# Two quads of state sums at a time, nine u tiles, and a front half worked off half by half

## The chip, the cores and the metric

The kernel runs on one core of a Trainium2 chip. The core has a matrix engine (TensorE, PE in the profile), a vector engine (VectorE, DVE), a scalar engine (ScalarE, ACT), a pool engine (GpSimd, POOL) and a queue that issues transfers (SyncE, SP). The metric is the time on the device in microseconds. Before the change it is 3439.42 us, the median of three runs that lie between 3437.82 and 3448.25 us.

## The reference: what is computed

Eight images of 384 channels and 32 x 32 = 1024 positions go through one layer. The first half of it is a state space block ("Mamba" style), followed by a two-layer perceptron; the second half is a feed-forward part with sign-binarised weights and outputs scaled by a maximum over one image. Cut to what matters:

```
t = layernorm(layernorm_c(x)) * ln_w + ln_b
xm, z = split(t @ in_proj_w.T)                    # 2 x 768 columns
xc = silu(conv3(xm) + conv_b)                     # causal, 3 taps
dt, Bm, Cm = split(xc @ x_proj_w.T, [24, 40])     # 24 + 16 + 16 columns
dt = softplus(dt @ dt_proj_w.T + dt_proj_b)       # 768 columns
h_t = exp(dt_t * A) * h_(t-1) + dt_t * xc_t * B_t # 768 x 16 states, 1024 steps
y_t = sum over the 16 states of h_t * C_t
y = (y + xc * D) * silu(z)
t = gelu((y @ out_proj_w.T) @ mlp_w1.T + mlp_b1) @ mlp_w2.T + mlp_b2
x = x + t
# feed-forward, for the first five images; the others get zeros from it
h = quantise(layernorm(x) @ sign(W1 - mean).T + b1)    # maximum over the image
x = x + quantise(gelu(h) @ sign(W2 - mean).T + b2)
```

All arithmetic is in fp32.

## The kernel before

The program first writes down every operation of all images with its reads, writes and an estimated cost. A list scheduler (`Plan.run`) then plays the operations through a model of the five queues, and the order in which it takes them becomes the fixed order of instructions on each engine. Every buffer belongs to a ring of so many slots; an operation can be placed only when a slot is free in the model. When the model's TensorE would be idle for over 0.7 us it places small "spare" products with no use but to keep that engine running.

```
MM = 0.86          # model's cost of one 128x128x512 fp32 product (two passes)
SWITCH = 0.34      # model's cost of going over to the state sums and back
BATCH = 1          # quads of states that are summed at a time
SLACK = 1.0        # added in the model to what waits for the sums
...
"front": ring("front", 2), "t_f": ring("t_f", 2), "w_f": ring("w_f", 4),
"dt_r": ring("dt_r", 3), "dtx_r": ring("dtx_r", 3), "u": ring("u", 6),
"da": ring("da", 2, psum), "y": ring("y", 1, psum),
"yg": ring("yg", 1), "hid": ring("hid", 2), "t_b": ring("t_b", 1), "w_b": ring("w_b", 4),
"w6": ring("w6", 2), "w6_n": ring("w6_n", 2), "res": ring("res", 3),
"mm": ring("mm", 3, psum),
```

**The scan** (`scan`, `scan_tile`). The 16 states of a channel are four quads of four. A tile holds 32 channels x 4 states on the 128 partitions and 1024 positions. ScalarE makes `da = exp(dt * A)`, GpSimd `u = dtx * B`, VectorE scans `h = da * h + u`, then VectorE (three tiles of four) or GpSimd (one of four) multiplies by C into `u`, and TensorE adds the four states of each channel with a 128 x 32 matrix of ones and zeros, `fold`:

```
for m in range(DI // per_unit):            # a unit: 2 tiles for each of 4 quads
    py = self.piece("y", [P, T], "py")
    ...
    for q in range(NQUAD):
        hcs = []
        for i, js in enumerate(tiles):
            self.scan_tile(hcs, ...)       # each takes one u tile until it is summed
        batch.append((q, hcs))
        if len(batch) < BATCH:
            continue
        def sums(py=py, batch=batch):
            for q, hcs in batch:           # 4 products of 512 columns for each quad
                for p0, hc in parts:
                    nc.tensor.matmul(py.real[p0 : p0 + DQ, :], self.fold, hc,
                                     start=(q == 0), stop=(q == NQUAD - 1))
        with self.plan.lane(-1):
            add("PE", SWITCH + BATCH * MM, sums, ...)
```

There are 6 x 12 units of whole images and 2 x 2 x 6 units of the first and last image, whose scan runs in two halves of 512 positions with the state carried over; 96 units, 384 quads.

**The front** (`s1`) of an image, each half of 512 positions:

```
ts = [normed(half) for half in range(2)]   # load, two norms in one, scale and bias
for half, cols in enumerate(HALVES):
    t = ts[half]
    # 6 times: in_proj product with weights from ring w_f, conv on ScalarE and VectorE
    # silu; store xc
    if half:
        gate(0)                            # z = silu of the other 6 in_proj products
    # x_proj product with self.x_w; store rows of B and C
    # 6 dt_proj products with self.dt_w; softplus; dtx = dt * xc on GpSimd; store both
    if half:
        gate(1)
```

Image 1 alone uses the rings t_n, w_b, yg and hid for its front. Constants that stay in memory for the whole program are `self.x_w` (128 x 768), `self.dt_w` (128 x 768) and `self.spread` (128 x 512), which copies a norm's scale to all partitions and feeds the spare products.

**The back** (`s3`): out_proj (`p_out`), first perceptron product with weights from w_b (`p_h`), gelu, second product (`p_o`), residual in a `res` tile. **The feed-forward part** (`ffn`): `p_y<-tn` products with weights from w_b, each result through a `res` tile to memory, `p_y<-gf` products, two maxima by `quant_scale`, which spreads a column over a diagonal:

```
def spread_out():
    nc.vector.tensor_reduce(m1.real, mx.real, AX.X, ALU.max)
    nc.vector.tensor_scalar_mul(diag.real, self.ident, m1.real)
add("DVE", 0.4, spread_out, ...)
```

Of the kernel before, what the change touches and what calls it, by code (L numbers as in the profile page):

```python
# [26 lines left out]
F32 = mybir.dt.float32  # L27
AF = mybir.ActivationFunctionType
# [42 lines left out]

MM = 0.86
SWITCH = 0.34
BATCH = 1
SIGNAL = 0.1
IDLE = 0.7
EARLY = 2
PATIENCE = 0.0
SLACK = 1.0
LOAD_TABLE = 1.29  # L80


def c_act(n):
    return 0.22 + n * 0.00084
# [233 lines left out]
class Layer:  # L318
    def __init__(self, ctx, tc, a, out):
        self.tc, self.nc, self.a, self.out = tc, tc.nc, a, out  # L320
        self.plan = Plan()

        def pool(name, **kw):
            return ctx.enter_context(tc.tile_pool(name=name, bufs=1, **kw))

        self.const = pool("const")
        sbuf, psum, dram = pool("sbuf"), pool("psum", space=PSUM), pool("dram", space=DRAM)

        def ring(tag, bufs, where=sbuf):
            def make(shape, name):  # L330
                return where.tile(shape, F32, tag=tag, name=name, bufs=bufs)

            return Ring(make, bufs)

        self.rings = {

            "front": ring("front", 2), "t_f": ring("t_f", 2), "w_f": ring("w_f", 4),
            "dbc": ring("dbc", 1), "halo": ring("halo", 2),

            "dt_r": ring("dt_r", 3), "dtx_r": ring("dtx_r", 3), "u": ring("u", 6),  # L340
            "xr": ring("xr", 1), "zr": ring("zr", 1), "state": ring("state", 1),
            **{f"bc{i}": ring(f"bc{i}", 1) for i in range(2 * NQUAD)},
            "da": ring("da", 2, psum), "y": ring("y", 1, psum),

            "yg": ring("yg", 1), "hid": ring("hid", 2), "t_b": ring("t_b", 1), "w_b": ring("w_b", 4),
            "w6": ring("w6", 2), "w6_n": ring("w6_n", 2), "res": ring("res", 3),

            "t_n": ring("t_n", 2), "small": ring("small", 12),

            "mm": ring("mm", 3, psum), "sq": ring("sq", 2),  # L350
            "rstd": ring("rstd", 2),
        }

        def handed(name, shape):
            return Fixed(dram.tile(shape, F32, name=name))

        self.dram = {}
        for b in range(B):
            for name in ("dt", "dtx"):
                self.dram[name, b] = handed(f"{name}_d{b}", [DI, L])  # L360

            for name in ("xc", "z", "yg"):
                self.dram[name, b] = handed(f"{name}_d{b}", [NP, P, T])
            self.dram["rows", b] = handed(f"rows_d{b}", [2 * NS, L])
            if b < NQ:
                self.dram["mid", b] = handed(f"mid_d{b}", [C, L])
                self.dram["y1", b] = handed(f"y1_d{b}", [P, KH, L])
        self.bin = {
            "W1": handed("bin_w1", [KH, P, KC, P]), "W2": handed("bin_w2", [KC, P, KH, P]),
        }  # L370
        self.constants()

        self.plan.spare = self.piece("mm", [P, T], "spare")
        self.plan.fill = lambda: self.nc.tensor.matmul(
            self.plan.spare.real[:, : 2 * P], self.ones, self.spread[:, :2, :], start=True,
            stop=True,
        )

    def piece(self, ring, shape, name):
# [4 lines left out]
    def constants(self):  # L384
        nc, a, const = self.nc, self.a, self.const
        self.ones = const.tile([P, P], F32, name="ones")
        nc.vector.memset(self.ones, 1.0)
        self.ident = ident = const.tile([P, P], F32, name="ident")
        make_identity(nc, ident)

        self.fold = const.tile([P, DQ], F32, name="fold")
        nc.vector.tensor_reduce(
            self.fold, ident.rearrange("p (d n) -> p d n", n=SQ), AX.X, ALU.add
        )

        self.spread = const.tile([P, G, P], F32, name="spread")
        for g in range(G):
            nc.vector.tensor_copy(
                self.spread[:, g, :], ident[:, g * DQ : g * DQ + 1].to_broadcast([P, P])
            )  # L400
        self.edge = const.tile([P, KD, 2], F32, name="edge")
        self.eps_m = const.tile([P, 1], F32, name="eps_m")
        nc.vector.memset(self.eps_m, E1 * E2)
        self.eps_f = const.tile([P, 1], F32, name="eps_f")
        nc.vector.memset(self.eps_f, E_FFN)

        def vec(name, k):
            v = const.tile([P, k], F32, name=f"v_{name}")
            nc.scalar.dma_start(v, a[name])
            return v  # L410

        self.ln_w, self.ln_b, self.mlp_b2 = vec("ln_w", KC), vec("ln_b", KC), vec("mlp_b2", KC)
        self.conv_b, self.dt_b = vec("conv_b", KD), vec("dt_proj_b", KD)
        self.d_pair, self.d_unit = vec("D_pair", NP), vec("D", KD)
        self.mlp_b1 = vec("mlp_b1", KH)
        self.b1, self.b2 = vec("b1", KH), vec("b2", KC)
        self.conv_w = const.tile([P, KD, 3], F32, name="conv_w")
        nc.scalar.dma_start(self.conv_w, a["conv_w"])
        self.a_neg = const.tile([P, NJ * NQUAD], F32, name="a_neg")
        nc.scalar.dma_start(self.a_neg, a["A_log"])  # L420
        nc.scalar.activation(self.a_neg, self.a_neg, AF.Exp)
        nc.vector.tensor_scalar_mul(self.a_neg, self.a_neg, -1.0)
        self.x_w = const.tile([P, KD, P], F32, name="x_w")
        nc.scalar.dma_start(self.x_w, a["x_proj_w"])
        self.dt_w = const.tile([P, DI], F32, name="dt_w")
        nc.scalar.dma_start(self.dt_w, a["dt_proj_w"])

    def load(self, to, view, src, r=(), size=0, cost=0.4):  # L430
# [45 lines left out]
    def norm(self, t, eps, scale):  # L476
# [40 lines left out]

        def spread():
            for g in range(G):
                nc.tensor.matmul(  # L520
                    p_r.real[:, g * TG : (g + 1) * TG], self.spread[:, g, :], rstd.real,
                    start=True, stop=True,
                )

        add("PE", MM, spread, r=[rstd], w=[p_r])
# [6 lines left out]
    def s1(self, b):  # L532
# [31 lines left out]
                    )  # L564
            return t

        def gate(half):
            t = ts[half]
            z = self.piece(r_z, [P, KD, T], "z")
            for m in range(KD):  # L570
                w = self.weights(r_w, KC, a["in_proj_w"][KD + m])
# [6 lines left out]
                     r=[], w=all_z, table="silu")  # L578
            by_pair("z", half, z[0])

        ts = [normed(half) for half in range(2)]
        for half, cols in enumerate(HALVES):
            t = ts[half]


            xc = self.piece(r_x, [P, KD, T], "xc")
# [32 lines left out]
                     r=[], w=all_m, table="silu")  # L619
            by_pair("xc", half, xc[0])  # L620

            if half:
                gate(0)


            p_dbc = self.piece("mm", [P, T], "p_dbc")

            def x_proj(xc=xc, p_dbc=p_dbc):
                for k in range(KD):
                    nc.tensor.matmul(  # L630
                        p_dbc.real, self.x_w[:, k, :], xc.real[:, k, :],
                        start=(k == 0), stop=(k == KD - 1),
                    )

            dbc = self.piece("dbc", [P, T], "dbc")
            add("PE", KD * MM, x_proj, r=all_m, w=[p_dbc], claim=[dbc])
            add("ACT", 0.59, lambda dbc=dbc, p_dbc=p_dbc: nc.scalar.copy(dbc.real, p_dbc.real),
                r=[p_dbc], w=[dbc])
            d = self.dram["rows", b]
# [1 line left out]
                       4 * 2 * NS * T)  # L641
            dt = self.piece(r_x, [P, KD, T], "dt")
            for k in range(KD):
                i = k % DTC * DQ
                pd = self.piece("mm", [P, T], "p_dt")
                add("PE", MM / 2, lambda i=i, k=k, pd=pd, dbc=dbc: nc.tensor.matmul(
                    pd.real, self.dt_w[i : i + R, k * P : (k + 1) * P], dbc.real[i : i + R, :],
                    start=True, stop=True,
                ), r=[dbc], w=[pd], claim=[dt])
                self.act(  # L650
                    lambda k=k, dt=dt: dt.real[:, k, :], lambda pd=pd: pd.real, AF.Identity,
                    c_act(T), r=[pd], w=[dt[k]], bias=self.dt_b[:, k : k + 1],
                )
# [6 lines left out]
            all_dt = [dt[k] for k in range(KD)]  # L660
            self.store_all("dt", b, half, dt, all_dt)
            self.store_all("dtx", b, half, xc, all_m)
            if half:
                gate(1)

    def store_all(self, name, b, half, t, parts):
        d = self.dram[name, b]
# [124 lines left out]
    def scan_tile(self, hcs, cols, n, dt_r, dtx_r, bq, cq, state, half, on_pool):  # L792
# [22 lines left out]
            ), r=[da, u] + ([state[cols[0]]] if half else []), w=[to])  # L815
        if half == 0:
            c0, step = cols[0], cols[1] - cols[0]
            add("ACT", 0.25, lambda: nc.scalar.copy(
                state.real[:, c0 : c0 + step + 1 : step], to.real[:, :, n - 1]
            ), r=[to], w=[state[c0]])  # L820
        if on_pool:
            add("POOL", 2.36, lambda: nc.gpsimd.tensor_mul(u.real, u.real, spread(cq)),  # L822
                r=[cq], w=[u])
# [151 lines left out]
    def quant_scale(self, mx, n):  # L975
# [4 lines left out]
        q = self.piece("small", [P, 4], "q")  # L980
        diag, p_max = self.piece("sq", [P, P], "diag"), self.piece("mm", [P, P], "p_max")

        def spread_out():
            nc.vector.tensor_reduce(m1.real, mx.real, AX.X, ALU.max)
            nc.vector.tensor_scalar_mul(diag.real, self.ident, m1.real)

        add("DVE", 0.4, spread_out, r=[mx[k] for k in range(n)], w=[m1, diag])

        add("PE", 0.25, lambda: nc.tensor.matmul(
            p_max.real, self.ones, diag.real, start=True, stop=True  # L990
# [130 lines left out]
def _laid_out(i):  # L1121
# [25 lines left out]
        rows[k * DQ : k * DQ + R] = xw[:R]  # L1147
        a["dt_proj_w"][k * DQ : k * DQ + R] = dw.T
    rows[DTC * DQ :] = xw[R:]
    a["x_proj_w"] = rows.reshape(P, KD, P).transpose(2, 1, 0)  # L1150

    a["D_pair"] = np.tile(np.asarray(i[c + "D"]).reshape(NP, DP).T, (2, 1))
    w2 = blocks(i[c + "mlp_w2"])
# [29 lines left out]
```

## Time and profile before

| what | value |
|---|---|
| time, median of three | 3439.42 us |
| profiled span | 3444.9 us |
| busy PE, DVE, ACT, POOL | 3302.8, 2885.8, 2019.7, 2655.3 us |
| mean granted TensorE clock | 0.975 of full |
| moved by transfers | 746.30 MB, mean 217 GB/s |
| first and last scan instruction | 111.6 us, 3338.0 us |
| sums: instructions, busy | 3072, 427.9 us |
| spare products: instructions, busy | 522, 128.4 us |

One fp32 product is two instructions on TensorE. Their ends are modelled and overlap the next start, so the distance from one start to the next tells what a product costs, and the busy time overstates it. A group of instructions has one line with its count, its busy time, the mean of one, and the idle time of the engine just before it with what ended most of that. "L454" is the line of a helper that emits nearly all dense products; they are told apart by the names of the tiles. The table by stage that is used below is cut at the last operation of each image's scan, so each of its rows is the time in which one image is scanned while the other engines work on the front of a later image and the back of an earlier one.

### The profile page before, as it was taken

Reading aid. Unit: us, or ns where it says so; the run is one execution under the profiler, and the core shown is the slowest. Engines: PE = TensorE matmul, PEld = TensorE weight load, DVE = VectorE, ACT = ScalarE, POOL = GpSimd, SP = SyncE. Lnnn points to the kernel's source line nnn. Section 1 sums busy time; section 2 is a strip of 40 time slices with the busy share of each in tenths; the row PEclk is TensorE's granted clock in tenths of the full one; section 3 lists DMA queues with packets and bytes.
Section 4 is the critical chain, followed back from the end, with each engine's and each line's share of the span. In section 5 each row is a group of like instructions: output and inputs, shape, how many; then the busy total and the mean of one; then the engine's idle time right before and its main releaser. Section 6 shows DMA issues by size and latency. Waiting matters only on the chain.

```text
span 3444.9 us, 32879 instructions
## 1 busy us (share of the span) xinstructions
PE 3302.8 (96%) x10500; PEld 1326.3 (38%) x10500; DVE 2885.8 (84%) x2193; ACT 2019.7 (59%) x2295; POOL 2655.3 (77%) x1288
## 2 busy tenths in 40 slices
PE   8888898999999999999999999999899999999999
PEld 3333433434343334333333333333333433333344
DVE  3577789899899989789989989899998899789870
ACT  4676567556666565554565656655576554555541
POOL 1778777777897968689777888788898779878850
PEclk9889899999999999999999999999999999999999
DMA  5876757667686557765588665986577666766542
GB/s 192 259 237 210 242 179 231 200 207 248 228 285 200 198 191 259 240 215 188 206 270 278 221 204 184 304 248 215 177 269 250 199 201 208 238 190 206 182 138 69
DMA packets 363965, 746.30 MB, mean 217 GB/s; under 512 B 34832, under 2 KB 103952, under 8 KB 363792
## 3 DMA queue, kind: packets, MB, share of 16 engines
q1 hardware_dynamic: 361776, 743.31, 66.6%
q8 instruction: 84, 1.38, 0.2%
q10 hardware_dynamic: 2016, 0.88, 0.1%
q14 instruction: 89, 0.73, 0.1%
HBM read 560.56 MB, written 183.50 MB: 216 GB/s over the span
## 4 chain that ended last, share of the span: by engine, by line
PE 61%; DVE 12%; DMA 8%; ACT 8%; POOL 5%; issue 5%; SPq 1%; DVEq 0%; POOLq 0%; ACTq 0%
PE p_y L454 14%; PE p_o L454 11%; PE p_h L454 10%; PE py L745 7%; DVE da L812 7%; PE p_out L454 6%; PE p_in L454 4%; PE p_z L454 4%; ACT da L470 3%; POOL u L808 2%; DVE u L825 2%; PE p_dbc L630 2%; ACT L470 1%; PE p_sum L483 1%; DMA dt_r<-dt_d 1%
## 5 line engine op out<-in xcount | busy, mean ns | idle before, releaser
L808 POOL TENSOR_TENSOR u<-dtx_r,bc 128x1024 f32<-128x1024 f32 x768 | 1796.8, 2359 | 493.7 <-PE py L745 418.9
L812 DVE TENSOR_TENSOR_SCAN da<-da,u 128x1024 f32<-128x1024 f32 (+1 forms) x576 | 1163.9, 2021 | 187.3 <-ACT da L470 113.0
L470 ACT ACTIVATE da<-dt_r,a_neg 128x1024 f32<-128x1024 f32 (+1 forms) x960 | 903.1, 946 | 687.8 <-DVE u L825 571.8
L825 DVE TENSOR_TENSOR u<-da,bc 128x1024 f32<-128x1024 f32 x576 | 703.2, 1221 | 25.2 <-DVE da L812 0.9
L454 PE MATMUL p_h<-t,w_b 128*128 128x512 f32 x1152 | 519.9, 601 | 12.2 <-ACT g L470 9.4
L454 PE MATMUL p_o<-g,w 128*128 128x512 f32 x1152 | 513.8, 598 | 1.2 <-DMA w<-in_mlp_w 1.0
L822 POOL TENSOR_TENSOR u<-u,bc 128x1024 f32<-128x1024 f32 x192 | 452.7, 2358 | 66.6 <-DVE u L812 46.1
L745 PE MATMUL py<-u,fold 128*32 128x512 f32 x3072 | 427.9, 611 | 15.7 <-POOL u L822 15.4
L812 DVE TENSOR_TENSOR_SCAN u<-da,u 128x1024 f32<-128x1024 f32 (+1 forms) x192 | 384.3, 2011 | 45.8 <-ACT da L470 29.8
L454 PE MATMUL p_y<-gf,w_n 128*128 128x512 f32 x720 | 328.9, 610 | 12.7 <-DMA w_n<-bin_w 8.2
L454 PEld LDWEIGHTS p_h<-t,w_b 128*128 128x128 f32 x1152 | 212.2, 190 | 315.0 <-issue 252.0
L454 PE MATMUL p_y<-tn,w_b 128*128 128x512 f32 x720 | 328.4, 605 | 1.0 <-ACT dt L470 0.8
L454 PEld LDWEIGHTS p_o<-g,w 128*128 128x128 f32 x1152 | 213.6, 190 | 299.9 <-issue 288.2
L470 ACT ACT_TABLE_LOAD x223 | 286.1, 1283 | 8.4 <-DVE xc L601 4.7
L454 PE MATMUL p_out<-yg,w 128*128 128x512 f32 x576 | 267.3, 616 | 16.8 <-DMA yg<-yg_d 9.6
L454 PE MATMUL p_in<-t,w_f 128*128 128x512 f32 x504 | 232.3, 608 | 10.3 <-ACT halo L596 6.0
L454 PE MATMUL p_z<-t,w_f 128*128 128x512 f32 x504 | 231.1, 607 | 2.3 <-ACT dt L470 1.3
L454 PEld LDWEIGHTS p_y<-gf,w_n 128*128 128x128 f32 x720 | 136.2, 194 | 204.0 <-issue 186.4
L454 PEld LDWEIGHTS p_y<-tn,w_b 128*128 128x128 f32 x720 | 134.1, 192 | 192.4 <-issue 154.0
L812 DVE TENSOR_TENSOR_SCAN da<-da,state,u 128x512 f32<-128x512 f32 x144 | 185.0, 1284 | 19.0 <-ACT da L470 7.0
L470 ACT ACTIVATE y<-p_y,v_b 128x512 f32<-128x512 f32 x150 | 101.8, 684 | 150.8 <-PE p_y L454 103.6
L601 DVE SCALAR_TENSOR_TENSOR xc<-p_in,conv_w,xc 128x511 f32<-128x511 f32 (+1 forms) x192 | 140.7, 742 | 54.2 <-ACT xc L470 32.6
(94 smaller groups left out, 2777.9 us busy)
## 6 DMA issues: line engine op xcount, KB each, us to landing
dtx_r<-dtx_d SPq DMA_DIRECT2D x144, 512.0 KB, 5.1
dt_r<-dt_d SPq DMA_DIRECT2D x144, 512.0 KB, 5.2
w_b<-in_mlp_w SPq DMA_DIRECT2D x192, 192.0 KB, 2.8
w<-in_mlp_w SPq DMA_DIRECT2D x96, 384.0 KB, 3.4
w_f<-in_in_proj_w SPq DMA_DIRECT2D x168, 192.0 KB, 4.5
y_d<-y SPq DMA_DIRECT2D x120, 256.0 KB, 3.8
gf<-y_d SPq DMA_DIRECT2D x20, 1536.0 KB, 9.2
xc_d<-xc SPq DMA_DIRECT2D x32, 768.0 KB, 7.5
```

Source lines behind the costliest of these rows:

```text
L454: self.nc.tensor.matmul(p.real, w.real[:, k, :], t.real[:, k0 + k, :], start=start and k == 0, stop=stop and k == n - 1,)
L470: lambda: self.nc.scalar.activation(out(), in_(), func, **{k: v() if callable(v) else v for k, v in kw.items()}),
L483: nc.tensor.matmul(p_sum.real, self.ones, t.real[:, k, :], start=(k == 0), stop=(k == KC - 1))
L601: nc.vector.scalar_tensor_tensor(xc.real[:, m, s:], pm.real[:, : T - s], tap[2 - s], xc.real[:, m, s:], ALU.mult, ALU.add,)
L630: nc.tensor.matmul(p_dbc.real, self.x_w[:, k, :], xc.real[:, k, :], start=(k == 0), stop=(k == KD - 1),)
L745: nc.tensor.matmul(py.real[p0 : p0 + DQ, :], self.fold, hc, start=(q == 0), stop=(q == NQUAD - 1),)
L808: add("POOL", 2.36, lambda: nc.gpsimd.tensor_mul(u.real, dtx_r.real, spread(bq)), r=[dtx_r, bq], w=[u])
L812: add("DVE", 0.13 + n * 0.0021, lambda k=k, col=col: nc.vector.tensor_tensor_scan(to.real[:, k, :], da.real[:, k, :], u.real[:, k, :], sta ...
L822: add("POOL", 2.36, lambda: nc.gpsimd.tensor_mul(u.real, u.real, spread(cq)), r=[cq], w=[u])
L825: add("DVE", 1.21, lambda: nc.vector.tensor_mul(u.real, da.real, spread(cq)), r=[da, cq], w=[u])
```

## The change

Its aim is to go over to the state sums half as often, by summing two quads at once, and to give the scan enough `u` tiles for that. The room for three more `u` tiles (12 KB of each partition) comes from `spread`, `x_w` and `dt_w`, which no longer stay in memory, and from one slot less in each of w_f, w_b and res. The weights of x_proj and dt_proj are loaded for every half image into the front's weight ring. The copies from `spread` are replaced by one column of the identity, read again and again. The front finishes one half (its gate too) before it starts the other. Two small operations go to another engine.

```
-BATCH = 1
+BATCH = 2
-SLACK = 1.0
+SLACK = 0.6
...
-            ... "w_f": ring("w_f", 4),
+            ... "w_f": ring("w_f", 3),
-            ... "u": ring("u", 6),
+            ... "u": ring("u", 9),
-            ... "w_b": ring("w_b", 4),
+            ... "w_b": ring("w_b", 3),
-            ... "res": ring("res", 3),
+            ... "res": ring("res", 2),
...
         self.plan.fill = lambda: self.nc.tensor.matmul(
-            self.plan.spare.real[:, : 2 * P], self.ones, self.spread[:, :2, :], start=True,
-            stop=True,
+            self.plan.spare.real[:, : 2 * P], self.ones,
+            self.ones.unsqueeze(1).to_broadcast([P, 2, P]), start=True, stop=True,
         )
...
-        self.spread = const.tile([P, G, P], F32, name="spread")
-        (four copies of a column of ident, one for each g)
-        self.x_w = const.tile([P, KD, P], F32, name="x_w")
-        self.dt_w = const.tile([P, DI], F32, name="dt_w")
-        (their two loads)
...
             for g in range(G):
+                one = self.ident[:, g * DQ : g * DQ + 1].to_broadcast([P, P])
                 nc.tensor.matmul(
-                    p_r.real[:, g * TG : (g + 1) * TG], self.spread[:, g, :], rstd.real,
-                    start=True, stop=True,
+                    p_r.real[:, g * TG : (g + 1) * TG], one, rstd.real, start=True, stop=True
                 )
...
-        ts = [normed(half) for half in range(2)]
         for half, cols in enumerate(HALVES):
-            t = ts[half]
+            t = normed(half)
...
-            if half:
-                gate(0)
...
-            add("PE", KD * MM, x_proj, r=all_m, w=[p_dbc], claim=[dbc])
+            for i in range(2):
+                w = self.weights(r_w, KC, a["x_proj_w"][i])
+                self.matmuls(p_dbc, w, xc, i * KC, KC, i == 0, i == 1, all_m, [dbc])
...
             for k in range(KD):
+                if k % KC == 0:
+                    w = self.weights(r_w, KC, a["dt_proj_w"][k // KC])
...
-            if half:
-                gate(1)
+            gate(half, t)
...
         if half == 0:      # state kept for the second half
-            add("ACT", 0.25, ... copy of the last column ...)
+            if on_pool:
+                add("POOL", 0.12, ... the same copy on GpSimd ...)
+            else:
+                add("ACT", 0.25, ... as before ...)
...
-            nc.vector.tensor_scalar_mul(diag.real, self.ident, m1.real)
+        self.act(lambda: diag.real, lambda: self.ident, AF.Identity, c_act(P), r=[m1], w=[diag],
+                 scale=lambda: m1.real)
```

More of the change, by code (lines that the diff above doesn't have):

```diff
@@ L335, in __init__ @@
         self.rings = {
-            "front": ring("front", 2), "t_f": ring("t_f", 2), "w_f": ring("w_f", 4),
+            "front": ring("front", 2), "t_f": ring("t_f", 2), "w_f": ring("w_f", 3),
             "dbc": ring("dbc", 1), "halo": ring("halo", 2),
-            "dt_r": ring("dt_r", 3), "dtx_r": ring("dtx_r", 3), "u": ring("u", 6),
+            "dt_r": ring("dt_r", 3), "dtx_r": ring("dtx_r", 3), "u": ring("u", 9),
             "xr": ring("xr", 1), "zr": ring("zr", 1), "state": ring("state", 1),
@@ L343, in __init__ @@
             "da": ring("da", 2, psum), "y": ring("y", 1, psum),
-            "yg": ring("yg", 1), "hid": ring("hid", 2), "t_b": ring("t_b", 1), "w_b": ring("w_b", 4),
-            "w6": ring("w6", 2), "w6_n": ring("w6_n", 2), "res": ring("res", 3),
+            "yg": ring("yg", 1), "hid": ring("hid", 2), "t_b": ring("t_b", 1), "w_b": ring("w_b", 3),
+            "w6": ring("w6", 2), "w6_n": ring("w6_n", 2), "res": ring("res", 2),
             "t_n": ring("t_n", 2), "small": ring("small", 12),
@@ L394, in constants @@
         )
-        self.spread = const.tile([P, G, P], F32, name="spread")
[L397 to L400, printed above, removed]
         self.edge = const.tile([P, KD, 2], F32, name="edge")
@@ L422, in constants @@
         nc.vector.tensor_scalar_mul(self.a_neg, self.a_neg, -1.0)
-        self.x_w = const.tile([P, KD, P], F32, name="x_w")
-        nc.scalar.dma_start(self.x_w, a["x_proj_w"])
-        self.dt_w = const.tile([P, DI], F32, name="dt_w")
-        nc.scalar.dma_start(self.dt_w, a["dt_proj_w"])
     def load(self, to, view, src, r=(), size=0, cost=0.4):
@@ L565, in normed, with gate @@
             return t
-        def gate(half):
-            t = ts[half]
+        def gate(half, t):
             z = self.piece(r_z, [P, KD, T], "z")
@@ L579, in gate @@
             by_pair("z", half, z[0])
-        ts = [normed(half) for half in range(2)]
         for half, cols in enumerate(HALVES):
-            t = ts[half]
+            t = normed(half)
             xc = self.piece(r_x, [P, KD, T], "xc")
@@ L620, in s1 @@
             by_pair("xc", half, xc[0])
-            if half:
-                gate(0)
             p_dbc = self.piece("mm", [P, T], "p_dbc")
[L628 to L633, printed above, removed]
             dbc = self.piece("dbc", [P, T], "dbc")
-            add("PE", KD * MM, x_proj, r=all_m, w=[p_dbc], claim=[dbc])
+            for i in range(2):
+                w = self.weights(r_w, KC, a["x_proj_w"][i])
+                self.matmuls(p_dbc, w, xc, i * KC, KC, i == 0, i == 1, all_m, [dbc])
             add("ACT", 0.59, lambda dbc=dbc, p_dbc=p_dbc: nc.scalar.copy(dbc.real, p_dbc.real),
@@ L643, in s1 @@
             for k in range(KD):
+                if k % KC == 0:
+                    w = self.weights(r_w, KC, a["dt_proj_w"][k // KC])
                 i = k % DTC * DQ
                 pd = self.piece("mm", [P, T], "p_dt")
-                add("PE", MM / 2, lambda i=i, k=k, pd=pd, dbc=dbc: nc.tensor.matmul(
-                    pd.real, self.dt_w[i : i + R, k * P : (k + 1) * P], dbc.real[i : i + R, :],
+                add("PE", MM / 2, lambda i=i, k=k, pd=pd, dbc=dbc, w=w: nc.tensor.matmul(
+                    pd.real, w.real[i : i + R, k % KC, :], dbc.real[i : i + R, :],
                     start=True, stop=True,
-                ), r=[dbc], w=[pd], claim=[dt])
+                ), r=[dbc, w], w=[pd], claim=[dt])
                 self.act(
@@ L817, in scan_tile @@
             c0, step = cols[0], cols[1] - cols[0]
-            add("ACT", 0.25, lambda: nc.scalar.copy(
-                state.real[:, c0 : c0 + step + 1 : step], to.real[:, :, n - 1]
-            ), r=[to], w=[state[c0]])
+            kept, last = lambda: state.real[:, c0 : c0 + step + 1 : step], n - 1
+            if on_pool:
+                add("POOL", 0.12, lambda: nc.gpsimd.tensor_copy(kept(), to.real[:, :, last]),
+                    r=[to], w=[state[c0]])
+            else:
+                add("ACT", 0.25, lambda: nc.scalar.copy(kept(), to.real[:, :, last]),
+                    r=[to], w=[state[c0]])
         if on_pool:
@@ L981, in quant_scale @@
         diag, p_max = self.piece("sq", [P, P], "diag"), self.piece("mm", [P, P], "p_max")
-        def spread_out():
-            nc.vector.tensor_reduce(m1.real, mx.real, AX.X, ALU.max)
-            nc.vector.tensor_scalar_mul(diag.real, self.ident, m1.real)
-        add("DVE", 0.4, spread_out, r=[mx[k] for k in range(n)], w=[m1, diag])
+        add("DVE", 0.17, lambda: nc.vector.tensor_reduce(m1.real, mx.real, AX.X, ALU.max),
+            r=[mx[k] for k in range(n)], w=[m1])
+        self.act(lambda: diag.real, lambda: self.ident, AF.Identity, c_act(P), r=[m1], w=[diag],
+                 scale=lambda: m1.real)
         add("PE", 0.25, lambda: nc.tensor.matmul(
@@ L1149, in _laid_out @@
     rows[DTC * DQ :] = xw[R:]
-    a["x_proj_w"] = rows.reshape(P, KD, P).transpose(2, 1, 0)
+    a["x_proj_w"] = rows.reshape(P, 2, KC, P).transpose(1, 3, 2, 0)
+    a["dt_proj_w"] = a["dt_proj_w"].reshape(P, 2, KC, P).swapaxes(0, 1)
     a["D_pair"] = np.tile(np.asarray(i[c + "D"]).reshape(NP, DP).T, (2, 1))
```

## The prediction

> **What bounds the kernel now.** I read the page's shares and slices first, then the chain that ended last, then a stretch of TensorE's timeline, then the table by stage. The page:
>
> ```profile
> PE 3302.8 (96%) x10500; PEld 1326.3 (38%) x10500; DVE 2885.8 (84%) x2193; ACT 2019.7 (59%) x2295; POOL 2655.3 (77%) x1288
> ...
> PE   8888898999999999999999999999899999999999
> ...
> DVE  3577789899899989789989989899998899789870
> ...
> PEclk9889899999999999999999999999999999999999
> ...
> PE 61%; DVE 12%; DMA 8%; ACT 8%; POOL 5%; issue 5%; SPq 1%; DVEq 0%; POOLq 0%; ACTq 0%
> ```
>
> TensorE is the bound through most of the span and has 61% of the chain. VectorE, with the scan, stands close behind; it is thin only in the first slices, where TensorE's clock is also lower. The busy time of TensorE overstates it, so I take distances between starts:
>
> ```profile
> 1101.38 10.57 PE L454 MATMUL p_o<-g,w 128*128 128x512 f32 x24
> 1111.88 1.06 PE L745 MATMUL py<-u,fold 128*32 128x512 f32 x8
> 1112.87 5.42 PE L454 MATMUL p_o<-g,w 128*128 128x512 f32 x12
> 1118.22 1.06 PE L745 MATMUL py<-u,fold 128*32 128x512 f32 x8
> 1119.22 1.12 PE L454 MATMUL p_o<-g,w 128*128 128x512 f32 x2
> ```
>
> From the start of 24 dense instructions to the sums are 10.50 us, from the start of 12 to the sums 5.35: 12 more cost 5.15, or 0.429 us each. One cycle of 12 and a block of sums is 1119.22 - 1112.87 = 6.35 us, so the block costs 6.35 - 5.15 = 1.20 us. Its eight instructions are four products side by side on quarters of the array, in two passes, which should be 2 x 0.429 = 0.86. **The other 0.34 us is the price of going over and back.** The 384 blocks never stand next to each other in the trace.
>
> Counting every start-to-start distance at its full-speed size, the needed products make 2967 us and the switches 384 x 0.34 = 131 us. That is 3098 of 3436 us from first to last product; about 340 us are waits, low clock and spare products. Where these are, the table by stage shows (columns: stretch, length, then busy time of PE, PEld, DVE, ACT, POOL; one row is the start, the scan of image 0, of image 3, of image 7):
>
> ```profile
> 0.00:112.00 112.00, 97.34 (x313) 42.25 (x314) 47.23 (x60) 58.10 (x85) 26.86 (x21) 0.94 0.67 223
> 112.00:610.00 498.00, 444.11 (x1425) 183.53 (x1426) 390.17 (x347) 335.10 (x461) 392.41 (x208) 0.92 0.71 221
> ...
> 1419.00:1804.00 385.00, 376.11 (x1200) 145.04 (x1198) 344.27 (x239) 227.34 (x231) 323.26 (x157) 0.98 0.68 222
> ...
> 2973.00:3346.00 373.00, 361.70 (x1086) 137.04 (x1085) 328.94 (x291) 211.63 (x315) 294.87 (x136) 1.00 0.60 185
> ```
>
> The scan of image 0 takes 498 us against 373 to 406 of the others, at a clock of 0.92; later TensorE is full and VectorE has 30 to 45 us to spare in each image.
>
> **What the Trainium skill says.** "TensorEngine Tiling (Array Packing)", Key Properties: a change of the tiling mode, and not of the tile alone, drains the engine. The trace agrees: the 0.34 us occur between a 128-wide and a 32-wide product, while the four tiles of one pass follow each other within 7 ns. "SBUF — State Buffer", The DMA setup-cost knee: about 2 us and bytes over 436 GB/s. For a 192 KB weight tile that makes an estimate of 2.45 us; the trace has 2.2 at the least, and medians of 2.8 and 4.5, because other transfers are under way. "TensorE: Matmul & The Clock Gate", Part 1, says that the clock is halved after an idle window; the table agrees (0.92 where TensorE starves). "SBUF — State Buffer", Who interferes with whom, says that a `tensor_scalar` of VectorE can be locked out by GpSimd; the ten `diag` instructions take 286 to 2493 ns for 128 columns, which fits.
>
> **The change, part by part.**
>
> *Two quads at a time.* 384 blocks become 192 of twice the size. The streaming stays (8 products, four passes, 1.72 us), one pair of switches in two goes: 192 x 0.34 = 65 us of TensorE time. In stretches where TensorE is the bound this is time; where the scan is, it turns into waiting. From the table I judge TensorE to be the bound in about three quarters to four fifths of the span: **-50 us**.
>
> *Nine u tiles.* These lines show why they are needed, and which loads lose a slot:
>
> ```profile
> L808 POOL TENSOR_TENSOR u<-dtx_r,bc 128x1024 f32<-128x1024 f32 x768 | 1796.8, 2359 | 493.7 <-PE py L745 418.9
> ...
> w_b<-in_mlp_w SPq DMA_DIRECT2D x192, 192.0 KB, 2.8
> ...
> w_f<-in_in_proj_w SPq DMA_DIRECT2D x168, 192.0 KB, 4.5
> y_d<-y SPq DMA_DIRECT2D x120, 256.0 KB, 3.8
> ```
>
> GpSimd waits 419 us for the sums to free a u tile. It is mostly harmless: VectorE itself waits only 81 us for u (65.4 and 16.0 in the waits by engine). Of six tiles two are held for a sum and four lie ahead; of nine, four are held and five lie ahead. A tile takes VectorE 2.28 + 3/4 x 1.22 = 3.2 us, so the run-ahead grows from 12.8 to 16 us, while each wait for TensorE's queue comes half as often. I count nothing for it, neither gain nor loss.
>
> *Half by half.* The first scan begins at 111.6 us, behind both halves' norms. The second half's norm has in that stretch on ScalarE 3 squares of 0.62, 3 scalings of 0.80, a root of 0.37 and two table loads of 1.28, some 7 us, and on VectorE 1.75 + 0.94 + 1.75 = 4.4 us. They lie partly in gaps of the first half's chain; behind the first half's dt they no longer can delay it. The gate's z for the first half also comes earlier. I count **-10 us**. Later images have their front done long before it is needed, so there I count nothing.
>
> *One slot less for weights and results.* A weight tile of w_f or w_b feeds six instructions, 6 x 0.429 = 2.57 us. With four slots the load can run 7.7 us ahead of its use, with three 5.15. In the trace the time from landing to first use, with loads and products paired in order, has a median of 7.6 us for the w_b tiles of `p_h`, and 14 of 192 lie under 3 us; for w_f 15 of 168 lie under 3. Take one tile's time away and some 30 loads come late, by up to 2 us each, of which I take 20 us at most and 10 as likely. The third res slot: a y tile lives 7.7 us (median) from its first product to the landing of its store, so two allow one each 3.9 us, where the 24 tiles of an image now come every 2.6 to 3.7 us in most places. But other products fill that gap in most places: 120 tiles x 0.3 us x a tenth, about 4 us. Together **+14 us**.
>
> *Weights of x_proj and dt_proj per half image.* 16 x 2 x 384 KB are 12.6 MB, 1.7% of the traffic, 64 loads more; transfers occupy two thirds of their time. They stand in the w_f ring in order, so gate weights cannot be fetched while x_proj waits for its silu: 1 to 3 us in a half image, covered by other products except at the very start. **+3 us**.
>
> *Small moves.* Ten `diag` of 1.24 us leave VectorE for ScalarE (0.37 us there, by the root of the same size), 12 us in all, of which a part stands before p_max: -4. State copies on GpSimd: 24 of 0.19 us, -3 at most, since ScalarE and GpSimd each lose about 9 us in waits around them. Column-broadcast weights for p_r are 104 products; no page and no trace here shows their price, so 0. **-7 us**.
>
> Sum: -50 - 10 + 14 + 3 - 7 = -50 us, or 3389. The order of instructions is also planned anew with SLACK at 0.6, which allows less room behind sums; that cannot be worked out. A plan made for this change should rather gain a little from it: I take -6 and predict **3383 us**.
>
> **The rivals.** *The scan takes over as the bound.* VectorE is 84% busy and 86 to 90% within an image's row, and GpSimd needs 77%. If these set the pace, the 65 us become waits and spare products, and the time is near 3425. Against it: TensorE has five times VectorE's share of the chain. *The lost slots bite.* If landings stay as slow as 4.5 us in the front and SP, which issues in order, stands behind a load whose slot is not free, scan loads come late too; then +40 to +60 us eat the gain: 3430 to 3450. For it: the w_f median; against it: most w_f tiles wait tens of us before use. *The plan gets better than its parts.* Earlier start, fewer interruptions, fewer waits for low clock: the 498 us of image 0 shrink towards 440, and the time goes to 3320 to 3340. For it: 340 us that no product needs; against it: GpSimd carries 392 us in that stretch, a good part of it binarising weights, which the change leaves as it is.
>
> **Range and chances.** The middle has the switch time with three quarters of its worth. Low end: all 65 us and 45 of the start, 3330. High end: nothing gained net, 3440. So 3330 to 3440. Faster by over 2% means under 3370.6, only 12 us below my number: 0.39. Within 2%: 0.55. Slower by over 2% needs both the slots to fail and the plan to get worse: 0.06.
>
> **What would show it.** Right: blocks of 16 sum instructions, 192 of them, each costing 2.06 us by distance of starts; rows of 375 to 400 us per image down by 5 to 8; the first scan near 100 us; TensorE's busy time lower by some 60 us (its spare products aside). Wrong: spare products well over 522, or more idle before `py` and VectorE's wait for u beyond 81 us (scan as the bound); idle of PE before `p_h`, `p_in`, `p_z` with a weight load as its end, beyond the few us of now (slots); ScalarE waiting for `y_d` (res). I would be wrong by most if the scan of image 0 changed by over 50 us either way.

## The result, and the profile after

The changed kernel takes 3409.88 us (median of four, 3402.08 to 3412.91), the kernel before 3443.03 us in the same runs: a ratio of 0.990, with a 95% interval of 0.9875 to 0.9925. That is 33 us less, where 56 less were predicted; it lies inside the range.

First the page of the changed kernel: shares, the slices, the chain, and the groups and loads that answer to those shown of before.

```profile
PE 3215.0 (94%) x10350; PEld 1327.0 (39%) x10350; DVE 2873.8 (84%) x2179; ACT 2015.3 (59%) x2277; POOL 2658.4 (78%) x1312
...
PE   8787898899989999899999999999998999999999
...
PEclk9898899999999999999999999999999999999999
...
PE 69%; DMA 9%; ACT 7%; DVE 7%; POOL 3%; issue 3%; SPq 1%; POOLq 0%; DVEq 0%; ACTq 0%
...
L788 POOL TENSOR_TENSOR u<-dtx_r,bc 128x1024 f32<-128x1024 f32 x768 | 1794.7, 2363 | 342.9 <-PE py L725 282.8
...
w_b<-in_mlp_w SPq DMA_DIRECT2D x192, 192.0 KB, 2.9
...
w_f<-in_in_proj_w SPq DMA_DIRECT2D x168, 192.0 KB, 4.6
y_d<-y SPq DMA_DIRECT2D x120, 256.0 KB, 3.4
```

TensorE has 88 us less of busy time, of which 36 are spare products (372 instructions with 91.9 us, against 522 with 128.4). VectorE and GpSimd are as before, and the chain has become more TensorE's, 69% against 61%. The weight loads land as fast as before by their medians. GpSimd waits 283 us for the sums instead of 419.

The timeline of TensorE, in the same part of the program:

```profile
1099.65 6.17 PE L443 MATMUL p_o<-g,w 128*128 128x512 f32 x14
1105.75 1.92 PE L725 MATMUL py<-u,fold 128*32 128x512 f32 x16
1107.61 5.42 PE L443 MATMUL p_o<-g,w 128*128 128x512 f32 x12
...
1112.86 10.46 PE L443 MATMUL p_out<-yg,w 128*128 128x512 f32 x24
1123.25 1.92 PE L725 MATMUL py<-u,fold 128*32 128x512 f32 x16
1125.11 5.42 PE L443 MATMUL p_out<-yg,w 128*128 128x512 f32 x12
```

The sums now come in blocks of 16 instructions, 192 in all. From the start of the 24 to that of the next 12 are 1125.11 - 1112.86 = 12.25 us; 24 dense instructions are 24 x 0.429 = 10.30, and one more 0.1 us is lost at the first instruction after the block in both kernels, so a block costs 2.05 us. Two blocks of before cost 2.40. Between the two quads of a block nothing is lost.

The table by stage, for the start and the scans of images 0, 3 and 7 (columns as in the table of before; the last three are TensorE's mean granted clock, the busy share of the DMA engines and GB/s):

```profile
0.00:112.00 112.00, 93.36 (x293) 39.34 (x294) 36.45 (x43) 55.96 (x81) 33.30 (x23) 0.91 0.71 233
112.00:599.00 487.00, 416.88 (x1341) 172.03 (x1339) 393.94 (x356) 328.56 (x446) 391.36 (x219) 0.90 0.72 229
...
1388.00:1768.00 380.00, 362.18 (x1176) 143.72 (x1174) 339.19 (x226) 223.62 (x220) 314.66 (x155) 0.97 0.68 223
...
2928.00:3308.00 380.00, 369.89 (x1134) 149.74 (x1132) 332.71 (x294) 216.72 (x311) 303.75 (x151) 1.00 0.61 188
```

The start is as long as before. The scan of image 0 is 11 us shorter, the others by 3.9 us on average (387.0 against 390.9 over images 1 to 7), which is less than the 5 to 8 us for each image that were predicted. From image 1 to 7 the rows change by -8, -12, -5, +2, +9, -20 and +7 us: single rows move by more than the gain, and three of them the other way. So the table does not show where the gain lies.

Last the waits of TensorE, after (what waited, for what, us in total, times, longest):

```profile
PE p_dbc L443 <- ACT xc L459: 16.8, 6, 8.5
...
PE p_z L443 <- DMA w_f<-in_in_proj_w: 12.4, 4, 6.0
PE p_in L443 <- DMA w_f<-in_in_proj_w: 11.5, 6, 4.0
...
PE p_h L443 <- DMA w_b<-in_mlp_w: 9.9, 7, 3.2
```

Before, the same waits, of which that of `p_in` does not occur:

```profile
PE p_dbc L630 <- ACT xc L470: 4.6, 3, 3.0
...
PE p_h L454 <- DMA w_b<-in_mlp_w: 2.0, 1, 2.0
...
PE p_z L454 <- DMA w_f<-in_in_proj_w: 0.3, 1, 0.3
```

**The three waits for weights, 34 us against 2, are new.**

The same sum for all runs. I split the time from the first to the last product into the needed products at full speed (2967 us in every run), the switches (blocks x 0.336), the spare products, what the low clock adds, and the rest, which are waits on TensorE. The first two kernels:

| | first to last product | switches | spare | low clock | waits |
|---|---|---|---|---|---|
| before | 3435 | 129 | 161 | 59 | 119 |
| after | 3396 | 65 | 122 | 66 | 177 |

The switches give 64 us, as worked out. Spare products, low clock and waits together go from 339 to 365, so 26 us are given back. The border between the last two columns is soft, by some 20 us, since a product that is both late and slow can be booked in either; their sum is not.

### The profile page after: what moved, and what is told of

Its sections match the earlier page's. It is cut to its first block, busy times and chain, and to the rows that moved or that the text cites. A ratio compares the mean times of both kernels' runs of the same rounds, so it can differ in the third digit from the quotient of the medians.

```text
span 3405.9 us, 32559 instructions
## 1 busy us (share of the span) xinstructions
PE 3215.0 (94%) x10350; PEld 1327.0 (39%) x10350; DVE 2873.8 (84%) x2179; ACT 2015.3 (59%) x2277; POOL 2658.4 (78%) x1312
## 2 busy tenths in 40 slices
DMA packets 372890, 758.06 MB, mean 223 GB/s; under 512 B 35824, under 2 KB 113136, under 8 KB 372720
## 4 chain that ended last, share of the span: by engine, by line
PE 69%; DMA 9%; ACT 7%; DVE 7%; POOL 3%; issue 3%; SPq 1%; POOLq 0%; DVEq 0%; ACTq 0%
PE p_y L443 16%; PE p_o L443 11%; PE p_h L443 11%; PE py L725 7%; PE p_z L443 6%; PE p_out L443 6%; PE p_in L443 5%; DVE da L792 4%; DMA w_f<-in_in_proj_w 2%; ACT da L459 2%; POOL u L788 2%; PE p_sum L472 2%; ACT L459 2%; PE p_dbc L443 1%; PE spare L374 1%
## 5 line engine op out<-in xcount | busy, mean ns | idle before, releaser
L788 POOL TENSOR_TENSOR u<-dtx_r,bc 128x1024 f32<-128x1024 f32 x768 | 1794.7, 2363 | 342.9 <-PE py L725 282.8
L443 PE MATMUL p_o<-g,w 128*128 128x512 f32 x1152 | 506.9, 595 | 2.5 <-DMA w<-in_mlp_w 2.5
L725 PE MATMUL py<-u,fold 128*32 128x512 f32 x3072 | 384.1, 606 | 16.1 <-POOL u L806 16.1
L443 PE MATMUL p_z<-t,w_f 128*128 128x512 f32 x504 | 234.9, 614 | 21.2 <-DMA w_f<-in_in_proj_w 12.4
L459 ACT ACTIVATE g<-p_h,v_mlp_b 128x512 f32<-128x512 f32 x192 | 127.7, 680 | 113.6 <-PE p_h L443 113.4
L725 PEld LDWEIGHTS py<-u,fold 128*32 128x32 f32 x3072 | 82.0, 109 | 281.7 <-issue 185.1
```

Source lines behind the costliest of these rows:

```text
L443: self.nc.tensor.matmul(p.real, w.real[:, k, :], t.real[:, k0 + k, :], start=start and k == 0, stop=stop and k == n - 1,)
L459: lambda: self.nc.scalar.activation(out(), in_(), func, **{k: v() if callable(v) else v for k, v in kw.items()}),
L725: nc.tensor.matmul(py.real[p0 : p0 + DQ, :], self.fold, hc, start=(q == 0), stop=(q == NQUAD - 1),)
L788: add("POOL", 2.36, lambda: nc.gpsimd.tensor_mul(u.real, dtx_r.real, spread(bq)), r=[dtx_r, bq], w=[u])
```

## The experiments

The theory to test: the time comes from the halved switches, and the lost weight slots give back a part. Rivals: the u tiles or the order of the front made the gain, or a new plan alone moves the time as much. All ratios are to the kernel before, measured on the same chip, with 95% intervals.

**One quad at a time.**

```
-BATCH = 2
+BATCH = 1          # all else as in the changed kernel
```

> The changed kernel with one quad at a time again; everything else of the change stays (nine u tiles, three weight slots, two res slots, half by half). Switch theory: 384 blocks of 8 come back, 64 us more of switching, of which the spare products and waits absorb some: 3445 to 3475 us, against 3410. Rival (the u tiles or the new plan made the gain, not the summing): 3400 to 3420, with as many spare products as the kernel before or more.

Measured: 3488.94 us, ratio 1.0136 (1.0115 to 1.0156). There are 380 blocks again, 128 us of switches; spare, low clock and waits are 380 us, close to the 365 of the changed kernel. The time is above the range that was expected of the switches; the rival's 3400 to 3420 us are far off, and so are its 522 or more spare products (464). Look where the time shows. The last scan ends at 3273 us, earlier than in the changed kernel (3301), but the program goes on for another 211 us, against 105 there. In that tail:

```profile
3273.00:3485.00 212.00, 203.26 (x474) 89.24 (x472) 7.95 (x11) 38.61 (x42) 3.61 (x2) 0.98 0.32 97
```

TensorE (203 of 212 us) works off what it could not do during the scan, and the others have little left (VectorE 8 us, ScalarE 39, GpSimd 4). The switches are a burden of TensorE, and it is the bound. So the switch theory holds in this pair of plans, with more than was expected of it; a second pair stands below.

**Two quads without the tiles.**

```
-BATCH = 1
+BATCH = 2          # in the kernel before, six u tiles
```

> The kernel before with two quads at a time and its six u tiles; nothing else of the change. If the u tiles are needed (four held, only two ahead), VectorE's wait for u from GpSimd grows from 81 us to 200 or more and the time is 3470 to 3550. Rival (the run-ahead does not matter, TensorE's switches do): 3370 to 3400, better than the change, since no slots are lost.

Measured: 3870.08 us, ratio 1.1242 (1.1218 to 1.1265), far above either expectation. The switches fall to 65 us, but the spare products rise to 610 us. VectorE's longest wait, then the group of spare products and that of u:

```profile
DVE da L812 <- POOL u L808: 370.3, 140, 16.5
```

```profile
L374 PE MATMUL spare<-spread,ones 128*128 128x256 f32 x2366 | 536.7, 384 | 0.3
```

```profile
L808 POOL TENSOR_TENSOR u<-dtx_r,bc 128x1024 f32<-128x1024 f32 x768 | 1792.4, 2358 | 816.2 <-PE py L745 693.0
```

GpSimd waits 693 us for the sums to free a tile, VectorE 427 us for u (370.3 and 56.8 in the two forms of the scan), and the model, which foresees it, keeps TensorE running with 2366 spare products. Two quads need the tiles; a TensorE at 94% busy hides that it has too little to do.

**Eight u tiles, and eight with four weight slots.**

```
-"u": ring("u", 9)
+"u": ring("u", 8)          # both runs
-"w_f": ring("w_f", 3)      -"w_b": ring("w_b", 3)
+"w_f": ring("w_f", 4)      +"w_b": ring("w_b", 4)      # the second run
```

> The changed kernel with eight u tiles instead of nine, the control for the next run. If four tiles ahead are enough, as before the change: 3405 to 3420. If the ninth tile carries part of the gain: 3425 to 3450, with a longer wait of VectorE for u.

> Eight u tiles, and the room of the ninth given back to the weights: four slots each of w_f and w_b. Theory that the lost slots gave back part of the gain: TensorE's waits for w_f and w_b loads fall from 34 us to under 8, and the time is 20 to 30 us below that of the run with eight u tiles alone. Rival (these waits would otherwise be others; the gain went to the order of the front): within 8 us of it.

Measured: 3474.63 us, ratio 1.0095 (1.0074 to 1.0117), and 3429.41 us, ratio 0.9962 (0.9950 to 0.9974). With eight tiles VectorE waits for u twice as long as with nine:

```profile
DVE da L792 <- POOL u L788: 100.3, 25, 13.6
```

against this in the changed kernel:

```profile
DVE da L792 <- POOL u L788: 43.5, 15, 7.9
```

The time with eight tiles is above both expectations. With the slots given back the three weight waits of TensorE fall from 31.5 us

```profile
PE p_h L443 <- DMA w_b<-in_mlp_w: 19.6, 9, 7.0
...
PE p_in L443 <- DMA w_f<-in_in_proj_w: 10.1, 4, 5.3
...
PE p_z L443 <- DMA w_f<-in_in_proj_w: 1.8, 2, 0.9
```

to 2.0:

```profile
PE p_in L443 <- DMA w_f<-in_in_proj_w: 1.5, 1, 1.5
...
PE p_h L443 <- DMA w_b<-in_mlp_w: 0.5, 1, 0.5
```

The whole of TensorE's waits falls from 208 to 175, and the time by 45 us, where 20 to 30 were expected. VectorE still waits 89.0 us for u in the second run, and is 45 us faster all the same. The slots cost something; how much of the 45 us is the new plan, the next runs limit.

**The old order of the front.**

```
+ts = [normed(half) for half in range(2)]
 for half, cols in enumerate(HALVES):
-    t = normed(half)
+    t = ts[half]
...
+    if half: gate(0, ts[0])         # ahead of x_proj
...
-    gate(half, t)
+    if half: gate(1, t)
```

> The changed kernel with the front's order of before: both halves' norms first, the gate of the first half ahead of the second half's x_proj, the gate of the second half at the end. If half by half was worth the 10 us of the prediction: 3415 to 3430, the first scan still near 112 us. Rival (that order costs: nothing fills TensorE while x_proj waits for its silu, 17 us of such waits after the change against 5 before): 3385 to 3405, with these waits at 6 us or less.

Measured: 3427.34 us, ratio 0.9948 (0.9928 to 0.9969). The first scan starts at 108.3 us, 3.6 us earlier than half by half, and the wait of x_proj for its silu stays (19.5 us). The time lies where the first theory put it, but what it gave as the reason, a later start, is not there, and neither is the rival's shorter wait. The 0.5% lie inside the scatter that follows.

**How much a new plan alone moves.**

```
-SIGNAL = 0.1       # model's time from one engine to another
+SIGNAL = 0.11      # or 0.09: only the order differs, and the spare products with it
```

> The changed kernel with the model's signal time at 0.11 instead of 0.10 us: no buffer, no operation and no cost on the chip differs, only the order that the scheduler finds. It measures how much a new plan alone scatters. If single steps of 30 us and more mean something: within 15 us of 3410. Rival (a new plan alone moves the time as much as the steps studied here): 25 us or more off.

> The changed kernel with the signal time at 0.09 us: a second new plan. If replanning scatters by some 20 us: between 3400 and 3445, most likely above the changed kernel. Rival (0.11 was an outlier): within 8 us of it.

> The kernel before with the model's signal time at 0.11 instead of 0.10 us: a new plan, nothing else. The same step moved the changed kernel up by 0.6%. If the plans as they stand are both picked ones: also 10 to 30 us above the kernel before. Rival (only the change's plan was picked): within 8 us of the kernel before, and then the change as such is worth less than the 1% measured.

> One quad at a time in the changed kernel, with the signal time at 0.11: a second plan of the run with one quad at a time. If the 79 us that one quad at a time cost were the switches: again 50 to 80 us above the changed kernel with the signal time at 0.11. Rival (a bad plan): 10 to 30 us above it.

Measured:

| kernel | as it is | 0.11 | 0.09 |
|---|---|---|---|
| before | 1 | 1.0079 (1.0059 to 1.0099) | |
| after | 0.9900 (0.9875 to 0.9925) | 0.9960 (0.9944 to 0.9975) | 1.0036 (1.0023 to 1.0049) |
| after, one quad | 1.0136 (1.0115 to 1.0156) | 1.0146 (1.0125 to 1.0168) | |

Each interval speaks of one plan. The changed kernel came out 21 us above its own first plan at 0.11, between the two expectations, and 47 us above it at 0.09, outside the range expected; the kernel before 27 us above, as for a picked plan. Between plans of the same kernel lie up to 1.4%, more than the whole change. The two kernels as they stand have the best plan of those tried. Means over plans: before 1.0040, after 0.9965, after with one quad 1.0141. The step between the last two is 1.8%, 60 us, and its plans do not overlap; at 0.11 alone it is 64 us, inside the 50 to 80 that the switches were to give. The rest of the change, from the first to the last, costs 1.0%, 35 us, and again the two pairs do not overlap. With two or three plans each these are rough sizes. The first step is well outside the scatter; the second rests on two plans against two, so that its sign is likely and its size open. What is left of the whole change is 0.75%, 26 us, by the means, and here the plans do overlap (1 to 1.0079 before, 0.9900 to 1.0036 after): the 33 us measured are those of two good plans, and a gain of the change as such is likely, but not shown.

Against the scatter, the single steps read so: eight tiles at 1.0095 lie above all three plans with nine, by 0.6 to 2.0%, but that is one plan, and eight tiles with four weight slots at 0.9962 lie among those with nine; the old front at 0.9948 lies among them too and shows nothing.

**Four weight slots with nine u tiles.** The room comes from one of the two sq tiles that hold the squares in a norm, so there is a control.

```
-"sq": ring("sq", 2)
+"sq": ring("sq", 1)        # both runs
-"w_f": ring("w_f", 3)      -"w_b": ring("w_b", 3)
+"w_f": ring("w_f", 4)      +"w_b": ring("w_b", 4)      # the second run
```

> The changed kernel with one sq tile instead of two, the control for the next run, which needs this room. The squares of a norm then alternate with their sums; 3410 to 3430.

> Nine u tiles and two quads as in the change, one sq tile, and four slots each of w_f and w_b. Theory that lost slots gave back part of the gain: TensorE's waits for w_f and w_b loads fall from 34 to under 8 us, and the time is 20 to 45 us below the control with one sq tile: 3370 to 3395. Rival (the 45 us found with eight u tiles were a lucky plan): within 15 us of the control.

Measured: 3456.30 us, ratio 1.0035 (1.0020 to 1.0050), and 3430.68 us, 0.9954 (0.9939 to 0.9968). Both are above the times expected; the step between them, 26 us, is within the 20 to 45 expected. The three weight waits, in the control:

```profile
PE p_h L443 <- DMA w_b<-in_mlp_w: 14.0, 7, 5.1
...
PE p_in L443 <- DMA w_f<-in_in_proj_w: 6.4, 5, 2.7
...
PE p_z L443 <- DMA w_f<-in_in_proj_w: 1.1, 1, 1.1
```

and with four slots:

```profile
PE p_h L443 <- DMA w_b<-in_mlp_w: 4.1, 2, 2.5
...
PE p_z L443 <- DMA w_f<-in_in_proj_w: 1.4, 1, 1.4
PE p_in L443 <- DMA w_f<-in_in_proj_w: 1.3, 1, 1.3
```

21.5 us become 6.8, and TensorE's waits together 155 instead of 208, while the time of the spare products rises from 138 to 159 us. Twice now, in two different surroundings, the time falls with the slots, by 0.8 and 1.3%. Each is one plan against one, and within the scatter of 1.4%; the two kernels with four slots (0.9962 and 0.9954) are no faster than the mean of the changed kernel's plans (0.9965).

The waits speak more clearly than the times, since all plans agree on them. The three weight waits together are:

| slots of w_f and w_b | plans | weight waits of TensorE, us |
|---|---|---|
| four | 5: the kernel before (two plans) and with two quads, the two runs with four slots | 2.0 to 8.2, mean 4.7 |
| three | 9: all others | 17.5 to 38.3, mean 30.0 |

So the lost slots bring some 25 us of waits, whatever the plan. That these are the bulk of the 35 us which the rest of the change costs is likely, and not shown.

**The model's SLACK.**

```
-SLACK = 0.6
+SLACK = 1.0
```

> The changed kernel with SLACK at 1.0 as before. If 0.6 is only one plan among others: 3410 to 3440, like the other new plans. Rival (less room behind the sums is a gain in itself): 3440 to 3470, with longer waits of GpSimd for the sums.

Measured: 3450.29 us, ratio 1.0020 (1.0010 to 1.0029). The time lies in the rival's range, but the longer waits that the rival named are not there (GpSimd waits 280.8 us for the sums, 282.8 in the changed kernel), and the ratio lies among the other plans. No worth of 0.6 by itself can be told.

No kernel of the study beats the changed one; the nearest are the four that lie between 0.9948 and 0.9962.

## Why the prediction was right, and where its steps were off

- *Switches, -50 of 65 us.* Right in mechanism and nearly in size. The block costs 2.05 us (2.06 predicted), TensorE saves 64 us, and by the means over plans 60 us of it reach the time. The scatter of the plans leaves open whether TensorE binds in more of the span than the three quarters to four fifths I took.
- *Nine u tiles, "neither gain nor loss".* Right for nine: VectorE's wait for u went from 81 to 53 us. The premise, that the waits behind the u tiles are mostly harmless, holds only while enough tiles lie ahead: VectorE waits 427 us for u with two ahead (one plan), 81 to 105 with four (four plans), 34 to 71 with five (seven plans) and 18 to 20 with seven (the two plans with one quad and nine tiles). Whether tiles come free two or four at a time makes no clear difference at four ahead (81 and 98 us against 105 and 89). What the ninth tile is worth in time is not shown: with three weight slots eight tiles are slower, with four they are not.
- *Half by half, -10 us.* Wrong. The first scan starts at 111.9 us as before (111.6), and with the old order at 108.3. So having both norms first did not hold the first scan up; that the second half's norm lay wholly in gaps of the first half's chain is likely, but was not traced.
- *Slots, +14 us: the mis-sized term.* I took 10 us for the weight slots and 4 for res. The weight waits of TensorE alone grew by 32 us, the plans with three slots wait 25 us more in the mean than those with four, and two pairs of runs put the slots at 26 and 45 us. My "some 30 loads late" was right, but "by up to 2 us each", of which I took half, was too short a delay: TensorE waited 17 times, 2.0 us in the mean and up to 6.0; after the change 27 loads of `p_h`, `p_in` and `p_z` are used within 0.5 us of landing, and these took a median of 6.3 us (w_b) and 8.9 us (w_f) to land, up to 12.4, against 2.8 and 4.2 for the others. Three slots let a load run 5.15 us ahead by my own sum, less than these slow landings take. The res slot cost about what I took: ScalarE waits 2.1 us for `y_d` (5.6 before), and TensorE 4.8 for ScalarE's `y`.
- *Weights of x_proj and dt_proj, +3.* Traffic is up by 11.8 MB, to 758.06: the 12.6 worked out, less the two loads of 384 KB at the start that fall away. The wait of x_proj for its silu went from 4.6 to 16.8 us in this plan, but stands at 19.5 with the old order too and at 3.1 with the signal time at 0.11, so its size belongs to the plan. No run takes this part, the res slot or the small moves back alone; what is left of the 35 us may lie there.
- *Small moves, -7.* `diag` takes 0.39 us on ScalarE (0.37 predicted, 1.24 on VectorE before). Column-broadcast weights cost nothing that shows: the median of a p_r product is 275 ns before and after. A state copy is 187 ns on GpSimd.
- *The plan, -6.* I treated it as a small gain; it is a scatter of up to 1.4% that no term of mine contains. The range of 110 us was wide enough for it, by luck more than by reckoning.
- *The sum.* I had all but the switches and the plan at nothing together (-10, +14, +3, -7); by the means over plans they cost 35 us. That, more than the switches, is why 56 us were too many. Two readings were a little off, without weight in the sum: VectorE has 35 to 47 us to spare in the rows of images 1 to 7, not 30 to 45, and is 88 to 91% busy there, not 86 to 90%.

Of the rivals, the scan as the bound does not fit (the two runs with one quad end with 211 and 194 us after the last scan; in the changed kernel spare products and VectorE's wait for u fell), and the lost slots did bite, with some 25 us of waits, and 26 and 45 us in the two pairs, where the rival named 40 to 60. The plan that is better than its parts did not come: the scan of image 0 takes 487 us, not near 440.

## What to carry to other kernels

An overhead per change of array mode can be cut by grouping, and was worth nearly its full size here, where the engine is the bound; but the group holds its inputs longer, so the run-ahead beside it must be bought first, and the price of where that room is taken belongs in the same sum. Price a slot by the slow landings, not by the median one. Where a scheduler fixes the order, measure a few plans of the same kernel before a per cent is read as the effect of a step.

## What the runs showed of the hardware that was not expected

Two groups of four 32-column products with the same weights follow each other at the pace of dense ones: 16 instructions in four passes span 1331 ns from first to last start, eight in two passes 473, and 473 + 2 x 429 = 1331. Weights read from one column of the identity, with the same column for all 128, load in the same 190 ns (185 to 333) as a full tile did (192). How long a 192 KB weight load takes to land goes with how many other loads and stores are under way when it is issued: in the kernel before, a median of 2.3 us with none (59 loads), 2.9 with two (59), 5.5 with four or more (132).
